# Layer 2's scores: the linear part of leaky relu as a sum per node, a one-operation relu, and a fixed order of three engines

## The chip, the cores and the metric

The kernel runs on one core of one Trainium2 chip. The metric is device time in microseconds (us): the median of several executions of the whole program, which holds four graph layers. One execution was also recorded by the hardware profiler; all views below are of that one.

## What is computed

The input x has 128 graphs of 64 nodes with 256 features. Four layers follow each other, each as `x = layernorm(x + layer(x))`. The change touches layer 2 and the end of layer 1 that is worked off beside it. Layer 2 is graph attention over 512 edges with four heads of 64 features:

```python
Xq = (H @ W_lin.T).reshape(bt, n, h, dh)
Xv = (H @ W_val.T).reshape(bt, n, h, dh)
e = jnp.einsum('behd,hd->beh', jax.nn.leaky_relu(Xq[:, src] + Xq[:, dst], 0.2), a)
e = e + jnp.log(A0[src, dst] + EPS)[None, :, None]
# softmax over the edges of one source, then
Y = segment_sum(attn[..., None] * Xv[:, dst], src)
out = Y @ W_out.T
```

The scores `e` need, for each graph, edge and head, a weighted sum over 64 features of a leaky relu. The last step of layer 1 is `x = layernorm(x + batchnorm(...))`; its batch norm is applied in a last pass over the nodes.

## The kernel before

**Tiles.** A tile of X holds two graphs: 128 partitions are 2 x 64 nodes, 256 features lie along the free axis. There are NT = 64 tiles. The scores take them as K = 32 pairs of tiles, in two halves of HU = 16 pairs; one half of the scores of one feature half `c` is one PSUM bank `sc`.

**One pair k of the scores** (`scores`, L2169) runs over these steps:

- `transposed(k)` (L2131) transposes the two tiles on TensorE into a bank `m`; VectorE copies it to `xT` (L2138).
- `maps(k)` (L2141) multiplies with the joint weights `wqv` (L2148, full 128x128 array): 256 columns are the queries, 256 the values. ScalarE copies the queries in a rounded form (`xh`, L2153), VectorE subtracts that from the bank to get the rest (`xl`, L2154), so that the edge matmuls can run as two passes of the fast float32 form. ScalarE copies the values to `xv` (L2165, two buffers), and SP's queue stores them to DRAM (L2166).
- `edges(c)` (L2182), once for each feature half: sixteen matmuls per pair (L2188, array split into 64x128) add the query vectors of the two ends of each edge, with the one-hot table `GG`. ScalarE copies each of four banks `l` to `xs` (L2194) and VectorE applies the leaky relu in place, `max(0.2 x, x)` (L2195).
- `products` (L2113) contracts `xs` over the features with the column table `az` (L2124, array split into 128x32, four at a time), and adds into `sc`.

**PSUM.** `m` has two banks, `l` two buffers of two banks each, `sc` two banks.

**What runs beside it.** In the first 16 pairs the last pass of layer 1 goes along as a generator `last_pass` (L2032): for each of 32 steps h, ScalarE applies the batch norm (`y`, L2039), TensorE transposes y back into a bank `m` (L2048), VectorE adds it to X (L1350), takes the statistics (L1353, L1354) and the root (`inv_sqrt`: a sum, ScalarE's square root at L1274, then a reciprocal, a product, a sum and a reciprocal on VectorE at L1275 to L1278, then the shift at L1365), and ScalarE scales X (L1369). Class `Norm` (L1337) holds this: `add` joins and collects, `flush` takes the root and scales. After pair 15 the softmax of the first half runs beside the scores, after that the fetch of its attention matrix `M` (L2285, on the queues of SP and GpSimd), and for the last seven pairs the first steps of `values` (mixing L2312, output map L2335). Layer 3 follows.

**What sets the order.** A scheduler orders each engine's instructions by its own estimate; `in_order` and `after` pin single ones. Semaphores between engines follow from the tiles that are read and written. Each engine then works its list strictly in order, and a queue issues its transfers in order.

## Time and profile before

| | us |
|---|---|
| median of 3 runs (2225.84 to 2228.0) | 2227.03 |
| the profiled execution, its time | 2226.54 |
| its span | 2224.8 |

Over the span TensorE is busy 2169.1 us (97%), VectorE 1831.2 (82%), ScalarE 940.3 (42%), GpSimd 162.9 (7%). By stages, busy us of each engine:

| stretch of the span, us | TensorE | VectorE | ScalarE | GpSimd |
|---|---|---|---|---|
| 0 to 1673, layers 0 and 1 | 1650.1 | 1397.8 | 546.9 | 79.5 |
| 1673 to 1840, scores with last pass | 163.3 | 144.1 | 139.2 | 1.8 |
| 1840 to 2026, scores with softmax and first values | 174.5 | 138.3 | 122.7 | 14.8 |
| 2026 to 2225, values and layer 3 | 181.2 | 151.0 | 131.4 | 66.7 |

In a line of the profile's groups or its timeline stand the engine, the line of the kernel, the operation, what it writes and reads, and sizes as partitions x elements. In the timeline, equal instructions that follow each other are merged (x4), the first two numbers are the start and the time from the first one's start to the last one's end, and a bracket gives the engine's idle time just before and what ended it. Float32 matmuls appear as two passes each.

### The profile page before, as it was taken

How to read it: one execution, taken by the hardware profiler on the slowest of the kernel's cores; microseconds unless marked ns; L12 is line 12 of the kernel's file. 1: busy time of each engine (PE TensorE's matmuls, PEld its weight loads, DVE VectorE, ACT ScalarE, POOL GpSimd, SP SyncE). 2: the span in 40 equal slices, each digit the busy share in tenths (PEclk: the TensorE clock that was granted, in tenths of full speed). 3: DMA queues.
4: the chain of work that ended last, by engine and by line, in shares of the span. 5: the costliest groups of instructions: out<-in, count | busy, mean ns of one | idle time of the engine just before them, and what ended most of it. 6: DMA issues, size and time to landing. Idle time of an engine off the chain costs nothing. (4 is left out here: it accounts for less than half of the span.)

```text
span 2224.8 us, 30044 instructions
## 1 busy us (share of the span) xinstructions
PE 2169.1 (97%) x8816; PEld 1212.6 (55%) x8816; DVE 1831.2 (82%) x9347; ACT 940.3 (42%) x1729; POOL 162.9 (7%) x196
## 2 busy tenths in 40 slices
PE   8999999999999999999999999999999999999997
PEld 6545665445665445665444654554434443446887
DVE  5788887888898899889899899787968888766788
ACT  1432322433322333332333222334437886667675
POOL 0111111101000000000000000000000000101532
PEclk9999999999999999999999999999999999999999
DMA  7000010111010111010111000012210010411522
GB/s 236 22 20 38 1 39 1 38 38 57 1 39 1 39 38 57 1 39 1 38 39 57 1 20 19 1 74 95 76 58 20 29 42 29 108 50 42 159 84 80
DMA packets 44668, 101.56 MB, mean 46 GB/s; under 512 B 5296, under 2 KB 23856, under 8 KB 43216
## 3 DMA queue, kind: packets, MB, share of 16 engines
q1 hardware_dynamic: 38384, 84.64, 11.0%
q0 software_dynamic: 3984, 14.40, 2.3%
q8 instruction: 70, 1.15, 0.2%
q10 hardware_dynamic: 2128, 0.54, 0.1%
q14 instruction: 102, 0.84, 0.1%
HBM read 67.97 MB, written 31.59 MB: 45 GB/s over the span
## 5 line engine op out<-in xcount | busy, mean ns | idle before, releaser
L1740 PE MATMUL pq<-H,wi 128*128 128x512 f32 (+1 forms) x1952 | 780.6, 540 | 1.5 <-ACT gate L1780 1.3
L1780 ACT ACTIVATE gate<-pq,bl 128x512 f32<-128x512 f32 (+1 forms) x504 | 315.8, 632 | 614.3 <-PE pq L1756 500.5
L1740 PEld LDWEIGHTS pq<-H,wi 128*128 128x128 f32 x1952 | 365.5, 190 | 336.8 <-issue 270.0
L1756 PE MATMUL pq<-lh,wh 128*128 128x512 f32 (+1 forms) x1152 | 461.3, 528 | 0.9 <-DVE lh L1798 0.8
L1756 PEld LDWEIGHTS pq<-lh,wh 128*128 128x128 f32 x1152 | 218.4, 190 | 202.5 <-issue 143.5
L1783 ACT ACTIVATE gate<-lc 128x512 f32<-128x512 f32 (+1 forms) x144 | 83.6, 581 | 278.8 <-DVE lc L1795 103.2
L2195 DVE SCALAR_TENSOR_TENSOR xs<-xs 128x512 f32<-128x512 f32 x256 | 165.3, 679 | 18.2 <-ACT xs L2194 15.1
L2194 ACT COPY xs<-l 128x512 f32<-128x512 f32 x256 | 135.6, 597 | 36.5 <-PE l L2188 30.4
L2148 PE MATMUL m<-wqv,xT 128*128 128x512 f32 (+1 forms) x264 | 123.1, 599 | 2.9 <-DVE xT L2138 1.3
L2012 PE MATMUL ps<-h,w 128*128 128x512 f32 x256 | 114.5, 604 | 5.0 <-ACT h L2006 2.7
L1369 ACT ACTIVATE X<-X,ln_sh,ln_rs 128x256 f32<-128x256 f32 x187 | 97.5, 594 | 37.1 <-DVE ln_sh L1365 21.2
L1958 PE MATMUL ps<-at,w 128*128 128x512 f32 x256 | 113.1, 593 | 0.0
L803 POOL PARTITION_ALL_REDUCE qQ<-qSG x62 | 74.0, 1193 | 508.5 <-DVE pc L135 268.9
L2012 PEld LDWEIGHTS ps<-h,w 128*128 128x128 f32 x256 | 48.3, 192 | 65.1 <-issue 55.1
L2148 PEld LDWEIGHTS m<-wqv,xT 128*128 128x128 f32 x264 | 46.0, 189 | 65.3 <-issue 39.8
L1958 PEld LDWEIGHTS ps<-at,w 128*128 128x128 f32 x256 | 47.2, 190 | 52.8 <-issue 51.4
L1353 DVE BATCH_NORM_STATS2 ln_st<-X 128x6 f32<-128x256 f32 x192 | 73.9, 415 | 1.2
L2124 PE MATMUL sc<-xs,az 128*32 128x512 f32 x512 | 74.5, 612 | 0.1
L131 DVE SCALAR_TENSOR_TENSOR CS<-GA,qE 64x1 f32<-64x1 f32 x294 | 61.8, 210 | 9.5
L1798 DVE TENSOR_TENSOR lh<-gate 128x512 f32<-128x512 f32 (+1 forms) x72 | 43.1, 602 | 31.5 <-ACT gate L1780 31.5
L131 DVE SCALAR_TENSOR_TENSOR GA<-qtg,CS,GA 64x1 f32<-64x1 f32 x294 | 61.6, 209 | 8.4
L1959 DVE BATCH_NORM_STATS2 st<-ps 128x6 f32<-128x512 f32 x64 | 43.8, 684 | 26.9 <-PE ps L1958 26.9
(637 smaller groups left out, 3452.0 us busy)
## 6 DMA issues: line engine op xcount, KB each, us to landing
wi<-in_WihT_dram SPq DMA_DIRECT2D x16, 1024.0 KB, 4.8
wh<-in_WhhT_dram SPq DMA_DIRECT2D x12, 1024.0 KB, 6.1
xd<-X SPq DMA_DIRECT2D x16, 512.0 KB, 2.6
X<-xd SPq DMA_DIRECT2D x16, 512.0 KB, 3.4
xv<-xv SPq DMA_DIRECT2D x32, 256.0 KB, 2.0
xr<-xv POOLq DMA_DIRECT2D x32, 256.0 KB, 3.0
X<-in_x_dram SPq DMA_DIRECT2D x15, 512.0 KB, 8.9
out_dram<-X SPq DMA_DIRECT2D x15, 512.0 KB, 2.9
```

Of the source, the lines that this page charges most:

```text
L131: self.nc.vector.scalar_tensor_tensor(o, a, s, b, op0, op1)
L1369: nc.scalar.activation(x, x, AF.Identity, bias=sh[:, k : k + 1], scale=rs[:, k : k + 1])
L1740: te.matmul(ps, wi[:, kk, o * P : (o + 1) * P], at(kk, k), start=(kk == 0), stop=(k == 0 and kk == 1))
L1756: te.matmul(ahead[gt, c], wh[:, kk, o * P : (o + 1) * P], hst[:, kk, :M], start=False, stop=(kk == 1))
L1780: s.activation(gates[gt][:, c, :M], ps, AF.Tanh if gt == 2 else AF.Sigmoid, bias=bl[:, p - 1, o : o + 1])
L1783: s.activation(*due.pop())
L1958: te.matmul(ps, w1[:, k, c * P : (c + 1) * P], at[:, k, :], start=(k == 0), stop=(k == 1))
L2012: te.matmul(ys[c], w2[:, k, c * P : (c + 1) * P], h[:, k, :], start=(k == 2), stop=(k == 1))
L2124: mms.append(te.matmul(sc[half][c][q : q + 32, :], az[:, c, HU - 1 - u_ : 3 * HU - 1 - u_], xs[b, i], start=(u_ == 0), stop=(u_ == HU - 1)))
L2148: te.matmul(pss[i][:, cols], xT[:, i, c, :], wqv[:, c, cols], start=(c == 0), stop=(c == 1))
L2194: taken.setdefault(i, []).append(s.copy(x, pl[:, b, :]))
L2195: ready.append(v.scalar_tensor_tensor(x, x, 0.2, x, ALU.mult, ALU.max))
```

## The change

The leaky relu is split as 0.8 relu(x) + 0.2 x. The factor 0.8 goes into `az`. The linear part needs no edges: for each node the queries are multiplied with the attention vector `a` on GpSimd (`arow`), summed per head on VectorE (`lin`), and once per half and feature half one matmul with the edge table adds 0.2 times these sums to the scores (`linear`). The relu is then one operation that reads PSUM: on ScalarE for the first graph of each tile (relu), on VectorE for the second (maximum with 0). Two more copies of the queries on ScalarE (`whole`) feed the sums.

`follow` ties each instruction of the scores to the one ahead of it on its engine, so that TensorE, ScalarE and VectorE work in the order in which the code stands. `last_pass` is no generator any more but hands out its parts, which `scores` places by hand: one pair is edges, transposes, maps, transposes, edges, and sixteen products, so the array changes its tile size four times a pair. `Norm` is split into `join`, `stats` and `root`, which returns the scalings to be placed later. Buffers: `xv` one instead of two, `xT` two instead of one, the queries' two parts three column blocks each instead of four buffers, `l` four single banks.

```diff
+    def root(self, dve=0):
+
+        nc, n, todo, mv = self.nc, len(self.todo), self.todo, self.mv
         rs = self.pool.tile([P, self.n], F32, tag="ln_rs", name="ln_rs")
...
+        return [lambda a=(k, t): scaled(*a) for k, t in enumerate(todo)]
...
-        y = normed(0)
-        for h in range(2 * NQ):
-            ps = pp.tile([P, 512], F32, tag="m", name="m")
+        y = {}
+
+        def turned(h):
+
+            ps, x = pp.tile([P, 512], F32, tag="m", name="m"), y.pop(h)
             for i in range(2):
                 for c in range(2):
-                    te.transpose(ps[:, i * D + c * P : i * D + (c + 1) * P], y[:, c, i * P : (i + 1) * P], ident)
-            with in_order(v, h < 3):
-                ln.add(2 * h, ps, 2)
+                    te.transpose(ps[:, i * D + c * P : i * D + (c + 1) * P], x[:, c, i * P : (i + 1) * P], ident)
+            ln.join(2 * h, ps, 2)
+
+        def prepare(h):
+
+            if h < 2 * NQ:
+                with in_order(s, True):
+                    y[h] = normed(h)
+
+        def whole(h):
+
+            with in_order(v, True):
+                turned(h)
+                ln.stats(2 * h, 2)
             if h == 1:
-                keep_awake(pg.tile([P, 2, 512], F32, tag="l", name="l")[:, 0, :], 2)
...
+                keep_awake(pg.tile([P, 512], F32, tag="l", name="l", bufs=4), 2)
+            prepare(h + 1)
+            with in_order(s, True), in_order(v, True):
+                ln.flush()
+
+        prepare(0)
+        return ln, turned, prepare, whole
...
-                v.tensor_tensor(az[:, c, o : o + 1], heads[:, h : h + 1], acol[:, c : c + 1], ALU.mult)
+                v.scalar_tensor_tensor(az[:, c, o : o + 1], heads[:, h : h + 1], 0.8, acol[:, c : c + 1], ALU.mult, ALU.mult)
+        arow = sx.tile([P, D], F32, tag="arow", name="arow", bufs=1)
+        ps = pp.tile([P, 512], F32, tag="m", name="m")
+        for c in range(2):
+            te.matmul(ps[:, c * P : (c + 1) * P], acol[:, c : c + 1].to_broadcast([P, P]), ident, start=True, stop=True)
+        v.tensor_copy(arow, ps[:, :D])
+        lin = sx.tile([P, 2, 2, 2, 2, HU], F32, tag="lin", name="lin", bufs=1)
+        linb = sx.tile([P, 2, 2, 2, 2, HU], F32, tag="linb", name="linb", bufs=1)
+        v.memset(linb, 0.0)
...
+        def follow(make, *a, eng=te, **k):
+
+            turn = next(i for i in reversed(nc.cur_bb.bb.instructions) if i.engine == eng.engine)
+            ins = make(*a, **k)
+            tc.add_manual_dep(ins.ins, turn.name, mybir.DependencyInfo(
+                mybir.DependencyClass.NoSync, mybir.DependencyReason.DATA), reason="turn")
+            return ins
+
+        def linear(half, c):
+
+            for b in range(2):
+                r = slice(b * N, (b + 1) * N)
+                v.tensor_scalar(linb[r, c, b], lin[r, half, c], 0.2, None, ALU.mult)
+            follow(te.matmul, sc[half][c], linb[:, c].rearrange("p b i h u -> p (b i h u)"), GG, start=False, stop=False)
...
+                if u_ == HU - 1:
+                    linear(half, c)
                 for b in range(2):
                     for i in range(2):
                         q = 32 * (2 * b + i)
-                        mms.append(te.matmul(sc[half][c][q : q + 32, :], az[:, c, HU - 1 - u_ : 3 * HU - 1 - u_],
+                        mms.append(follow(te.matmul, sc[half][c][q : q + 32, :], az[:, c, HU - 1 - u_ : 3 * HU - 1 - u_],
                                              xs[b, i], start=(u_ == 0), stop=(u_ == HU - 1)))
...
+                    follow(te.transpose, ps[:, i * D + c * P : i * D + (c + 1) * P], X[:, 2 * k + i, c * P : (c + 1) * P], ident)
+            xT = sx.tile([P, 2, 2, P], F32, tag="xT", name="xT", bufs=2)
...
+        parts = [[sx.tile([P, 3, P], F32R, tag=f"x{q}{i}", name=f"x{q}{i}", bufs=1) for q in "lh"] for i in range(2)]
+        sums, later = [], []
+
         def maps(k, xT, apart=False):
 
-            xq, xv = [], sx.tile([P, 2, D], F32, tag="xv", name="xv")
+            xq, whole, xv = [], sx.tile([P, 2, D], F32, tag="xq", name="xq", bufs=1), sx.tile([P, 2, D], F32, tag="xv", name="xv", bufs=1)
...
-                hi = sx.tile([P, D], F32R, tag="xh", name="xh", bufs=4)
-                lo = sx.tile([P, D], F32R, tag="xl", name="xl", bufs=4)
-                drawn[i] = s.copy(hi, pss[i][:, :D])
-                v.tensor_tensor(lo, pss[i][:, :D], hi.bitcast(F32), ALU.subtract)
+                lo, hi = (parts[i][q][:, :: k % 2 + 1][:, :2] for q in range(2))
+                x = pss[i][:, :D].rearrange("p (c d) -> p c d", c=2)
+                w = whole[:, i, :].rearrange("p (c d) -> p c d", c=2)
+                drawn[i] = follow(s.copy, hi, x, eng=s)
+                follow(s.copy, w, x, eng=s)
+                follow(v.tensor_tensor, lo, w, hi.bitcast(F32), ALU.subtract, eng=v)
                 xq.append((lo, hi))
...
                 product(i, slice(D, 2 * D) if apart else slice(0, 2 * D))
                 if not apart:
                     first(i)
-                s.copy(xv[:, i, :], pss[i][:, D:])
+                follow(s.copy, xv[:, i, :], pss[i][:, D:], eng=s)
+                nc.gpsimd.tensor_tensor(whole[:, i, :], whole[:, i, :], arow, ALU.mult)
+                yield
+            sums.append(lambda: follow(
+                v.tensor_reduce, lin[:, k // HU, :, :, :, k % HU].rearrange("p c i h -> p i c h"),
+                whole.rearrange("p i (c h d) -> p i c h d", c=2, h=2), AX.X, ALU.add, eng=v))
             nc.sync.dma_start(xvd[k], xv)
-            return xq
+            yield xq
 
         def scores():
 
 
             K = NT // 2
             xT = transposed(0)
-            xq = maps(0, xT, True)
-            next(beside[0])
-            next(beside[0])
+            *_, xq = maps(0, xT, True)
+            whole(2)
             xT = transposed(1)
 
+            def scales(n):
+
+                with in_order(s, True):
+                    while n and later:
+                        later.pop(0)()
+                        n -= 1
 
             held = {}
 
             def edges(c):
                 xs, ready = {}, []
                 for i in range(2):
-                    pl = pg.tile([P, 2, 512], F32, tag="l", name="l")
+                    pl = [pg.tile([P, 512], F32, tag="l", name="l", bufs=4) for _ in range(2)]
                     for part, b in ((0, 0), (0, 1), (1, 0), (1, 1)):
                         r = slice(b * N, (b + 1) * N)
-                        mm = te.matmul(pl[:, b, :], xq[i][part][r, c * P : (c + 1) * P], GGr[r, :],
+                        mm = follow(te.matmul, pl[b], xq[i][part][r, c, :], GGr[r, :],
                                        start=(part == 0), stop=(part == 1))
                         if not b and not part:
                             after(mm, taken.pop(i, []) + ([drawn[i]] if c == 0 else []))
                     for b in range(2):
                         x = xs[b, i] = sx.tile([P, E], F32, tag="xs", name="xs", bufs=10)
-                        taken.setdefault(i, []).append(s.copy(x, pl[:, b, :]))
-                        ready.append(v.scalar_tensor_tensor(x, x, 0.2, x, ALU.mult, ALU.max))
+                        y = (follow(v.tensor_scalar, x, pl[b], 0.0, None, ALU.max, eng=v) if b
+                             else follow(s.activation, x, pl[b], AF.Relu, eng=s))
+                        taken.setdefault(i, []).append(y)
+                        ready.append(y)
                 held[k, c] = xs, ready
-                last.append(mm)
 
             for k in range(K):
-                apart, xn = k < NQ, None
+                hb, ha = (h if h < 2 * NQ else None for h in (2 * k + 3, 2 * k + 4))
                 edges(0)
-                if apart:
-                    run(*beside)
-                    if k:
-                        products([(k - 1, 1)], held)
-                if k < K - 1:
-                    xn = maps(k + 1, xT)
-                if apart:
-                    run(*beside)
-                elif k < K - 2:
+                while sums:
+                    sums.pop()()
+                if ha:
+                    prepare(ha)
+                scales(2)
+                steps = maps(k + 1, xT) if k < K - 1 else iter((None,) * 3)
+                if k < K - 2:
                     xT = transposed(k + 2)
+                if hb:
+                    with in_order(v, True):
+                        turned(hb)
+                        ln.stats(2 * hb, 2)
+                next(steps)
+                scales(2)
+                next(steps)
+                xn = next(steps)
+                if ha:
+                    with in_order(v, True):
+                        turned(ha)
                 edges(1)
+                if ha:
+                    with in_order(v, True):
+                        ln.stats(2 * ha, 2)
+                products([(k - 1, 1), (k, 0)] if k else [(k, 0)], held)
+                if ha:
+                    prepare(ha + 1)
+                if hb:
+                    with in_order(v, True), in_order(s, True):
+                        later.extend(ln.root())
+                    if k in (0, NQ - 2):
+                        scales(4)
                 xq = xn
-                if apart:
-                    run(*beside)
-                    products([(k, 0)], held)
-                    xT = transposed(k + 2)
-                    run(*beside)
-                else:
-                    products([(k - 1, 1), (k, 0)], held)
                 if k == K - 1:
                     products([(k, 1)], held)
                 yield
...
+        sc_ = scores()
+        ln, turned, prepare, whole = last_pass()
+        whole(0)
+        whole(1)
         run(*[sc_] * (NQ - 1))
```

## The prediction

> **What bounds the kernel now.** I read the windows first, to see which engine is full in which stage, then the timeline of TensorE, VectorE and ScalarE for single pairs of layer 2's scores, then the waits of the DMA queue. The scores run from 1683 to 2026 us of the span. In their first half each pair also carries two steps of layer 1's last pass:
>
> ```profile
> core 0: us, PE busy (x) PEld busy (x) DVE busy (x) ACT busy (x) POOL busy (x), PEclk, DMA share, GB/s
> 1700.00:1750.00 50.00, 49.64 (x239) 20.27 (x237) 43.26 (x126) 43.56 (x100) 0.00 (x0) 1.00 0.06 22
> ```
>
> TensorE is busy 49.64 of 50 us and sets the pace; VectorE (43.3) and ScalarE (43.6) have some slack. The first maps of pairs 2 to 15 start at 1699.26 to 1839.41: thirteen periods in 140.15 us, 10.78 each. The timeline shows where one such period goes:
>
> ```profile
> 1742.56 1.98 PE L2148 MATMUL m<-wqv,xT 128*128 128x512 f32 x4
> 1744.47 0.50 PE L2188 MATMUL l<-edge_s,xl 64*128 64x512 f32 x2
> 1744.81 0.40 PE L2188 MATMUL l<-edge_s,xh 64*128 64x512 f32 x2
> 1745.04 0.39 PE L2188 MATMUL l<-edge_s,xl 64*128 64x512 f32 x2
> ...
> 1752.81 1.98 PE L2148 MATMUL m<-wqv,xT 128*128 128x512 f32 x4
> ```
>
> Edge matmuls follow each other 0.23 us apart (1744.81 to 1745.04), but the first couple after another tile size takes 0.34 (1744.47 to 1744.81). In this period the array's tile size changes ten times. The second half, without last pass, already has four changes a pair:
>
> ```profile
> 1884.83 0.50 PE L2188 MATMUL l<-edge_s,xl 64*128 64x512 f32 x2
> ...
> 1885.94 3.70 PE L2148 MATMUL m<-wqv,xT 128*128 128x512 f32 x8
> 1889.52 0.66 PE L2136 MATMUL m<-ident,X 128*128 128x128 f32 x4
> 1890.10 0.50 PE L2188 MATMUL l<-edge_s,xl 64*128 64x512 f32 x2
> ...
> 1891.23 1.92 PE L2124 MATMUL sc<-xs,az 128*32 128x512 f32 x16
> 1893.08 1.09 PE L2251 MATMUL m<-ident,se 128*128 128x128 f32 x8
> ```
>
> From starts: edges of one half E 1.12, maps M 3.58, transposes of X TX 0.58, sixteen products P 1.85; a y transpose TY beside other 128x128 work 0.52 (eight take 1.03).
>
> **Changes whose cost is plain.** *Tile order.* A first-half pair becomes E, TX, TY, M, TY, E, P: 1.12 + 0.58 + 0.52 + 3.58 + 0.52 + 1.12 + 1.85 = 9.3 us, 1.5 less than 10.78, if nothing waits. The second half keeps its order.
> *Elementwise work.* Eight copies (0.51 start to start) on ScalarE and eight operations L2195 (0.61) on VectorE become four relus and four maxima read from PSUM, plus two copies (0.27) on ScalarE and one reduction on VectorE. ScalarE: -8x0.51 + 4x0.55 + 2x0.27 = -1.3 us a pair. VectorE: -8x0.61 + 4x0.60 + 0.60 = -1.9. Neither bounds a pair now, so this alone gives nothing. A relu from PSUM is not in these rows; the gate row L1780 (128x512, 632 ns) and the copy L2194 (597) bound it. A maximum from PSUM lies between L1552 (from SBUF, 484 ns) and the copy L2138 (from PSUM, 677); I take L2138, 0.60 start to start. The reduction: L1551, 683 ns for the same 128x512.
> *GpSimd* gets two 128x256 products a pair (727 ns, row L2404). They end some 5 us before the reduction that waits for them; the DMA issues queued behind them on that queue are the scatters of the attention, which end about 0.2 to 1.5 us later.
> *The linear sum* adds four matmuls of 128x128x512 (two passes of 0.46): 0.9 us each, two before pair 17, two at the end: +2 at the end, and +1 net for pairs 14 to 24, where softmax operations now stand ahead of the xT copy but 2.8 us of TensorE idling on VectorE's backlog (0.52 + 0.51 + 0.46 + 1.28) shrink. The factor 0.8 in az costs nothing: same instructions.
>
> **The wait that the fixed order adds.** The two m banks are handed out in turn to TX, TY, M0, M1, TY: five uses a pair. M0, the first half of the maps, so takes the bank of the TX just before it, and the built program has it wait for that bank's reader, the copy xT for the pair after next. VectorE runs strictly: maximum, maximum, lin reduction, xT copy, join, statistics, lo, lo, join, maximum, maximum, statistics, then the six small operations of the normalization's root in a row. Before, the scheduler put those between other operations. Alone, they show their latency:
>
> ```profile
> 1676.27 0.17 DVE L1272 TENSOR_SCALAR is_t<-ln_mv 128x2 f32<-128x2 f32 x1
> 1676.71 0.17 DVE L1275 RECIPROCAL is_r<-is_s 128x2 f32<-128x2 f32 x1 [0.27 <-ACT is_s L1274]
> ...
> 1677.50 0.16 DVE L1365 SCALAR_TENSOR_TENSOR ln_sh<-ln_mv,ln_rs 128x2 f32<-128x2 f32 x1
> 1677.58 0.68 DVE L1350 TENSOR_TENSOR X<-m,X 128x512 f32<-128x512 f32 x1
> ```
>
> 1.31 us until the next operation (1676.27 to 1677.58), and 1.0 for two statistics and aggregates ahead of them (1675.27 to 1676.27). Now one loop, counted from the start of M0. M1 ends at 3.6. ScalarE's hi copy starts at 3.85, its second copy ends at 4.5. VectorE: second lo to 4.85, join to 5.45 (0.60), first maximum to 6.05. The second maximum and relu reuse xs buffers that the first four products of this pair still read: TensorE reaches P at 3.58 + 0.52 + 1.12 = 5.2 and eight passes take 1.06, so it runs from 6.3 to 6.9. Statistics to 7.9, root to 9.2, two maxima of the next E to 10.4, reduction to 11.0, xT copy to 11.7, semaphore 0.06: the next M0 starts at 11.8. TensorE had been ready at 9.3. So it idles 2.5 us a pair and VectorE's chain becomes the bound. Thirteen periods: 13 x (11.8 - 10.78) = **+13 us**. With the maxima at 0.48 and the reduction at 0.4 the period is 11.2, with 0.68 and 0.75 it is 12.2: +5 to +18.
>
> **The clock.** An idle stretch like this one has a price in the trace:
>
> ```profile
> 1664.72 5.40 PE L2012 MATMUL ps<-h,w 128*128 128x512 f32 x8 [2.19 <-issue]
> 1666.00:1668.00 2.00, 2.00 (x3) 0.66 (x2) 1.59 (x7) 0.20 (x1) 0.00 (x0) 0.50 0.02 4
> ```
>
> After 2.19 us idle the granted clock was 0.50, and eight matmuls that took 3.70 us just before took 5.40: 1.7 us lost. An idle of 2.73 us (before 1549.99) brought no drop, so it depends on how the idle lies in a recurring period. The drops begin whole multiples of 3.41 us apart in the records (the one at 1664.84 us, the later ones at 1948.15 and 2043.72). If 2.19 us must fall into one such period, 2.5 us of idle does so in (3.41 + 2.5 - 2x2.19)/3.41 = 45% of pairs; if 1.6 us is enough (1.56 at 1620 us was not), in 79%. The slow clock then falls on M, which is in the loop: 13 x 0.45 x 1.7 = **+10**, up to +17; none if the chain is shorter. [...]
>
> **Start.** The three whole steps ahead run their roots in VectorE's order: two of 1.31 us more stand before an xT copy than did, and the first loop's wait: M0 of pair 1 some 4 us later (0 to 5): **+4**.
>
> **One xv buffer instead of two.** The waits name the price:
>
> ```profile
> 1927.20 2.39 SPq L2285 DMA_DIRECT2D M<-attn_d  x4
> 1929.69 21.05 SPq L2166 DMA_DIRECT2D xv<-xv  x3
> 1948.88 0.37 ACT L2165 COPY xv<-m 128x256 f32<-128x256 f32 x1 [4.45 <-DMA xv<-xv]
> 1949.30 1.12 PE L2136 MATMUL m<-ident,X 128*128 128x128 f32 x4 [3.62 <-ACT xv L2165]
> ```
>
> The store of pair 24's xv stands behind the fetch of M on SP's queue and lands at about 1948.9. With two buffers pair 26 waited for it, 4.45 us. With one, pair 25 does. Its copy would start 2.5 us after its maps (1932.98), so it waits about 13 us, and the relus behind it on ScalarE hold the edge banks. TensorE still has E and P, then idles some 10.6 instead of 3.6: **+7** (0 if the store lands early, 10 at most). The slow clock after it is there in both.
>
> **Values.** In pairs 27 to 31 a join, statistics and every second time a root (0.6 + 1.0, + 1.3) stand ahead of the maxima and the xT copy, on which here M1 waits: copy done at 4.2 or 5.5 us after E starts, TensorE there at 3.5. Mean stall 1.4, less the 0.45 that present waits beyond yT's cost: +0.95 x 5 = **+5** (0 to 7). After 2026 us TensorE is the bound in both.
>
> **Sum.** 4 + 13 + 10 + 1 + 7 + 5 + 2 = +42 on the span of 2224.8; the run lay 1.7 above its span (2226.5), and the median of the runs is 2227.0: 2227 + 42 = **2269 us**.
>
> **Rivals.**
> A, *faster*: the xT copy comes in time, TensorE stays the bound at 9.3 us. Then 13 x (9.3 - 10.78) = -19 and start, clock and values cost nothing: -19 + 1 + 7 + 2 = -9, 2218 us. For it: VectorE's and ScalarE's sums fall. Against: the loop from the second lo to M0 would have to shrink from 7.3 to 4.8 us. It decides from a period of 10.0, which earns the 10 us of the rest (10.78 - 10/13).
> B, *the chain without the clock*: 11.3 us and no drop: 4 + 7 + 1 + 7 + 5 + 2 = +26, 2253. For it: 2.73 us once went free.
> C, *the slow clock nearly each pair, often for two periods of 3.41 us* (as at 1948): 13 x 0.8 x 3.3 = 34 for 10: 2293.
> D, *it does not do what it says*, the stall eating just the saved changes: period 9.7, -14 + 15: 2228.
>
> **How the numbers follow.** Forecast 52% (its own range 2258 to 2280), B 22%, C 14%, A 8%, D 4%. The range reaches into B and C: 2240 to 2290. Under 0.2% (about 4.5 us) a measurement of this kernel can't tell a change from none: faster 0.08, same 0.03, slower 0.89.
>
> **What would show it.** Right: PE idle of 2 to 3 us before each M0 of the first half, released by the xT copy; periods near 11.8 to 13.5; PEclk 0.5 in part of the slices; one xv wait of 12 us or more on ScalarE. Wrong: first-half periods under 10.5, or the xT copy ending before TY does; a first half that is warm and a loss that lies in the second.

## The result, and the profile after

| | before | after |
|---|---|---|
| median, us (range) | 2227.5 (2225.8 to 2228.5) | 2281.3 (2277.2 to 2285.5) |
| the profiled execution, its time | 2226.54 | 2277.24 |
| its span | 2224.8 | 2275.5 |

The changed kernel is slower: the ratio is 1.0242, with a 95% interval of 1.0223 to 1.0262. The prediction was 2269, with a range of 2240 to 2290; the 2281.3 lies inside it, and just above the 2258 to 2280 that the forecast gave as its own.

The windows of the changed kernel, cut at the same steps as the table of before (layers 0 and 1; scores with last pass; scores with softmax and values; the rest), with the start of pair 15's maps as the second cut. Columns: length, busy time of each engine, granted clock, DMA.

```profile
core 0: us, PE busy (x) PEld busy (x) DVE busy (x) ACT busy (x) POOL busy (x), PEclk, DMA share, GB/s
0.00:1673.00 1673.00, 1649.93 (x5136) 900.82 (x5136) 1398.00 (x8155) 547.00 (x886) 79.55 (x76) 1.00 0.11 39
1673.00:1882.80 209.80, 167.43 (x783) 82.13 (x783) 134.81 (x384) 122.97 (x288) 23.70 (x33) 0.87 0.07 25
1882.80:2078.20 195.40, 175.73 (x1089) 81.55 (x1087) 106.45 (x212) 93.26 (x214) 38.70 (x52) 0.97 0.20 56
2078.20:2275.50 197.30, 181.56 (x1824) 162.04 (x1824) 149.92 (x514) 131.32 (x275) 67.07 (x99) 0.97 0.35 99
```

The scores' first half took 209.8 us instead of 167, the second 195.4 instead of 186, the last stage 1.5 us less. In the first half TensorE works nearly as long as before (167.4 against 163.3 us, part of it now at half the clock), but with 42 us of gaps around it, and VectorE and ScalarE, whose work fell by 9 and 16 us, are idle more than before. So no engine is full: a chain of waits sets the pace. And the granted clock is 0.87, where it was 1.00.

The timeline of TensorE shows one period (in the records of this kernel all operations that went through `follow` carry line 2150, so one reads them by their tiles):

```profile
1762.49 5.40 PE L2150 MATMUL m<-wqv,xT 128*128 128x512 f32 x8 [2.52 <-DVE xT L2150]
...
1771.23 0.50 PE L2150 MATMUL l<-edge_s,xl 64*128 64x512 f32 x2
...
1772.36 0.66 PE L2150 MATMUL m<-ident,X 128*128 128x128 f32 x4
1772.85 0.60 PE L2066 MATMUL m<-ident,y 128*128 128x128 f32 x4
1775.97 5.40 PE L2150 MATMUL m<-wqv,xT 128*128 128x512 f32 x8 [2.52 <-DVE xT L2150]
...
1816.46 3.70 PE L2150 MATMUL m<-wqv,xT 128*128 128x512 f32 x8 [2.52 <-DVE xT L2150]
```

In the pair shown TensorE has its transposes done at 1773.4 and then idles 2.52 us, as in every pair from 3 to 15, until the xT copy frees the bank. The eight map matmuls then take 5.40 us instead of 3.70. A period, from the start of one pair's maps to the start of the next pair's, is 13.48 us here (1762.49 to 1775.97). Of pairs 3 to 15, pair 10's maps (1816.46) alone have the full clock, and the next maps start 11.78 us later, at 1828.24.

The timeline of VectorE over the same pair is the chain, from the second lo (`xl`, the rest of the second half's queries) to the xT copy:

```profile
1768.60 0.43 DVE L2150 TENSOR_TENSOR xl<-xq,xh 128x256 fp32r<-128x256 f32 x1 [2.00 <-ACT xq L2150]
1768.95 0.68 DVE L1353 TENSOR_TENSOR X<-m,X 128x512 f32<-128x512 f32 x1
1769.55 0.68 DVE L2150 TENSOR_SCALAR xs<-l 128x512 f32<-128x512 f32 x1
1770.50 0.69 DVE L2150 TENSOR_SCALAR xs<-l 128x512 f32<-128x512 f32 x1 [0.27 <-PE sc L2150]
1771.11 0.74 DVE L1362 BATCH_NORM_STATS2 ln_st<-X 128x6 f32<-128x256 f32 x2
1771.77 0.30 DVE L1363 BATCH_NORM_AGGREGATE ln_mv<-ln_st 128x2 f32<-128x6 f32 x2
1772.10 0.17 DVE L1272 TENSOR_SCALAR is_t<-ln_mv 128x4 f32<-128x4 f32 x1
...
1773.44 1.28 DVE L2150 TENSOR_SCALAR xs<-l 128x512 f32<-128x512 f32 x2
1774.64 0.68 DVE L2150 TENSOR_REDUCE lin<-xq 128x8 f32<-128x512 f32 x1
1775.23 0.68 DVE L2150 COPY xT<-m 128x512 f32<-128x512 f32 x1
```

From 1772.10 to 1773.44 stand the six small operations of the root, and in that time the maxima of the next pair wait, whose banks TensorE had filled by 1772.4. Behind the list's first line, which waits 2.00 us for ScalarE's copy of the maps, nothing in it waits long for another engine (0.27 us at the second maximum, and 0.27 us inside the root); it is simply a list.

The clock, in windows of 1 us over the same stretch:

```profile
1774.00:1775.00 1.00, 0.00 (x0) 0.00 (x0) 1.00 (x3) 1.00 (x3) 0.00 (x0) 1.00 0.00 0
...
1776.00:1777.00 1.00, 1.00 (x3) 0.52 (x4) 0.96 (x3) 0.00 (x0) 0.00 (x0) 1.00 0.00 0
1777.00:1778.00 1.00, 1.00 (x3) 0.49 (x2) 0.52 (x3) 0.00 (x0) 0.00 (x0) 0.52 0.00 0
1778.00:1779.00 1.00, 1.00 (x2) 0.34 (x2) 0.00 (x0) 0.18 (x1) 0.00 (x0) 0.50 0.00 0
...
1781.00:1782.00 1.00, 1.00 (x7) 0.63 (x7) 0.00 (x0) 0.60 (x3) 0.00 (x0) 1.00 0.00 0
```

The drop to 0.50 does not come in the idle stretch (1773.4 to 1776.0), but a microsecond after its end, when TensorE is busy again, and it lasts some 3.4 us. It falls on the maps, which are the next link of the chain.

Why pair 10 is spared shows in windows that are cut at the drops. Where the granted clock falls in this trace, it falls at whole multiples of 3.41 us from the other drops (1777.05, 1804.35 and 1828.25 are 8 and 7 multiples apart), and in pairs 3 to 15 it stays down for one such stretch. Here are pairs 7, 9 and 10, each with the stretch of 3.41 us ahead of a possible drop and the stretch behind it:

```profile
1773.63:1777.05 3.42, 1.08 (x3) 0.60 (x4) 3.38 (x7) 1.81 (x4) 0.00 (x0) 1.00 0.00 0
1777.05:1780.46 3.41, 3.41 (x6) 1.35 (x5) 0.89 (x4) 1.65 (x5) 0.46 (x1) 0.50 0.00 0
1800.94:1804.35 3.41, 1.38 (x3) 0.68 (x4) 3.38 (x9) 1.50 (x4) 0.00 (x0) 1.00 0.00 0
1804.35:1807.77 3.42, 3.42 (x5) 1.35 (x4) 0.59 (x3) 1.90 (x5) 0.73 (x1) 0.50 0.00 0
1814.59:1818.01 3.42, 1.55 (x4) 0.84 (x5) 3.38 (x9) 1.34 (x3) 0.00 (x0) 1.00 0.00 0
1818.01:1821.42 3.41, 3.41 (x18) 1.77 (x16) 0.84 (x3) 2.85 (x9) 0.73 (x1) 1.00 0.00 0
```

The idle is 2.52 us in all three pairs, but the part of it that lies inside one stretch shrinks from pair to pair: 2.34 us in pair 7, 2.03 in pair 9, 1.87 in pair 10 (3.42 less 1.55). After 2.03 us the clock halved, after 1.87 it did not.

By starts of the maps, after minus before, the whole +50.7 us of the span divides so: +9.0 at pair 2; +33.8 from pair 2 to 15; +2.7 from 15 to 25; +2.3 from 25 to 27; +4.4 from 27 to 31; -1.5 from there to the end.

### The profile page after: what moved, and what is told of

The parts are those of the page before. It is cut to its first block, busy times and chain, and to the rows that moved or that the text cites. A ratio compares the mean times of both kernels' runs of the same rounds, so it can differ in the third digit from the quotient of the medians.

```text
span 2275.5 us, 30057 instructions
## 1 busy us (share of the span) xinstructions
PE 2174.7 (96%) x8828; PEld 1226.5 (54%) x8828; DVE 1789.2 (79%) x9261; ACT 894.5 (39%) x1663; POOL 209.0 (9%) x260
## 3 DMA queue, kind: packets, MB, share of 16 engines
q1 hardware_dynamic: 38384, 84.64, 10.8%
## 5 line engine op out<-in xcount | busy, mean ns | idle before, releaser
L2150 PE MATMUL m<-wqv,xT 128*128 128x512 f32 (+1 forms) x264 | 146.9, 704 | 46.0 <-DVE xT L2150 42.3
L2150 PEld LDWEIGHTS m<-wqv,xT 128*128 128x128 f32 x264 | 56.3, 228 | 115.7 <-DVE xT L2150 57.0
L2150 DVE TENSOR_TENSOR xl<-xq,xh 128x256 fp32r<-128x256 f32 x64 | 27.7, 433 | 111.0 <-ACT xq L2150 110.4
L2150 DVE TENSOR_SCALAR xs<-l 128x512 f32<-128x512 f32 x128 | 84.7, 683 | 20.0 <-PE sc L2150 11.2
L2150 ACT ACTIVATE xs<-l 128x512 f32<-128x512 f32 x128 | 73.4, 598 | 46.7 <-PE sc L2150 25.6
L2221 POOL TENSOR_TENSOR xq<-xq,arow 128x256 f32<-128x256 f32 x64 | 47.0, 735 | 434.1 <-DVE xl L2150 434.1
```

What stands on the lines that cost most here:

```text
L2150: ins = make(*a, **k)
L2221: nc.gpsimd.tensor_tensor(whole[:, i, :], whole[:, i, :], arow, ALU.mult)
```

## The experiments

Unless said otherwise each is the changed kernel with one edit. Times between chips differ (the kernel before had medians of 2222 to 2228 us), so ratios to it on the same chip are given, and for parts the spans and the starts of the maps. Differences of spans carry that spread between chips, some 5 us; starts within one trace do not.

**TensorE's gap filled.** The transposes ahead of the maps are given several times, into the same bank from the same data; VectorE's list does not change.

```diff
-            for i in range(2):
+            for i in [0, 1] * n:
...
-                        turned(hb)
+                        turned(hb, 5 if k else 1)
```

> The changed kernel with the four transposes that stand just ahead of the maps in pairs 1 to 14 given five times instead of once (same bank, same data): they fill 2.1 of the 2.52 us in which TensorE idles before the first half of the maps. VectorE's chain is not touched. Theory (the idle itself costs nothing more than 11.78 - 10.78 a pair, the rest is the slow clock that it brings): period 11.8, the eight map matmuls 3.70 instead of 5.40 in every pair, granted clock 1.0 from 1682 to 1830: 12 x 1.7 = 20 us less, 2261. Rival 1 (the slow clock comes from something else in the pair, such as the array's tile sizes or VectorE's load): period stays 13.5, 2281. Rival 2 (transposes longer than the gap, M0 late): period above 11.8 with a full clock, 2265 or more.

The ratio was 1.0169 (1.0152 to 1.0186), the span 2257.8, 17.7 us less. Its TensorE timeline:

```profile
1778.55 2.35 PE L2066 MATMUL m<-ident,y 128*128 128x128 f32 x20
1781.66 3.70 PE L2150 MATMUL m<-wqv,xT 128*128 128x512 f32 x8 [0.77 <-DVE xT L2150]
...
1790.35 2.35 PE L2066 MATMUL m<-ident,y 128*128 128x128 f32 x20
1793.46 2.84 PE L2150 MATMUL m<-wqv,xT 128*128 128x512 f32 x6 [0.76 <-DVE xT L2150]
```

The period is 11.79 us (the mean of pairs 3 to 15), the maps of each of them take 3.70 us, the granted clock is 1.00 from 1720 to 1860, and the maps still start on the xT copy. More work for TensorE made the kernel faster. So the period of 13.49 is a chain of 11.78 and 1.71 of slow clock, and the slow clock comes from the gap. With three and with two times the transposes:

> The changed kernel with the same four transposes given three times instead of five, so that about 1.65 us of idle is left before the maps (0.77 with five, 2.52 with one). If an idle stretch must reach about 2.2 us within one period of 3.41 us of the throttle: no pair drops, period 11.8, 2261, as with five. If 1.4 us in such a period is enough (what 12 slow pairs of 13 would give for phases that fall at random), about two pairs in three drop, period 12.9 in the mean, 2275. If every idle over 1.2 us is enough: period 13.5, 2281.

Ratio 1.0154 (1.0137 to 1.0171), span 2258.4: with 1.65 us idle the maps of pairs 3 to 9 take 3.70 us each, and the span is within 0.6 us of that with five times the transposes.

> The changed kernel with the four transposes ahead of the maps given twice, which leaves about 2.1 us of idle (1.65 with three brought no slow pair, 2.52 with one brought 12 of 13). If at least about 2.2 us must fall into one period of the throttle: no slow pair, period 11.8, 2261. If the bound lies between 1.7 and 2.1: the idle meets it at some phases; a slow pair moves the phase by only 0.16 us, a warm one by 1.5, so slow pairs come in rows, 5 to 11 of 13, mean period 12.5 to 13.3, 2270 to 2279.

Ratio 1.0258 (1.0241 to 1.0275), no gain at all. Its timeline of TensorE:

```profile
1789.10 5.40 PE L2150 MATMUL m<-wqv,xT 128*128 128x512 f32 x8 [2.08 <-DVE xT L2150]
1802.58 3.70 PE L2150 MATMUL m<-wqv,xT 128*128 128x512 f32 x8 [2.08 <-DVE xT L2150]
1814.37 5.36 PE L2150 MATMUL m<-wqv,xT 128*128 128x512 f32 x8 [2.08 <-DVE xT L2150]
```

With 2.08 us idle, 11 of the 13 pairs 3 to 15 are slow (maps of 5.36 to 5.40 us instead of 3.70); the warm ones are pair 3 and pair 9, with five slow ones between. So the bound for these periods lies between 1.65 and 2.08 us, not at 2.19 as the prediction took it: 0.43 us of idle decide over some 20 us.

**The root taken later.** The root of pairs 1 to 13 is taken in the next pair, behind the join that follows the xT copy.

```diff
                         turned(hb)
+                        if 1 < k < NQ - 1:
+                            with in_order(s, True):
+                                later.extend(ln.root())
                         ln.stats(2 * hb, 2)
...
-                if hb:
+                if k in (0, NQ - 2):
                     with in_order(v, True), in_order(s, True):
                         later.extend(ln.root())
-                    if k in (0, NQ - 2):
-                        scales(4)
+                    scales(4)
```

> The changed kernel with the normalization's root of pairs 1 to 13 taken in the next pair, behind the join that follows the xT copy, so that its six small operations (1.3 us) no longer stand between the products and the next xT copy. Theory (VectorE's strict chain sets the pair): chain 11.78 - 1.3 = 10.5, TensorE idles about 1.2 us before the maps; if that idle no longer halves the clock, 12 x (13.49 - 10.5) = 36 us less, 2245; if it still does, period 12.2, 16 us less, 2265. Rival (the six operations only lie in a wait that is there anyway, for the scores' bank or the relus): period 13.5, no change, 2281.

Ratio 1.0094 (1.0078 to 1.0111), span 2239.5: 36.0 us less. The timeline of TensorE:

```profile
1762.37 3.70 PE L2150 MATMUL m<-wqv,xT 128*128 128x512 f32 x8 [1.11 <-DVE xT L2150]
1772.75 2.84 PE L2150 MATMUL m<-wqv,xT 128*128 128x512 f32 x6 [1.11 <-DVE xT L2150]
```

The period is 10.39, the idle 1.11 us, the granted clock 1.00 (1720 to 1840). Six operations of 0.16 to 0.18 us each, moved behind the xT copy, are worth 3.1 us a pair: 1.39 of chain and 1.71 of clock.

**The transposes of X moved behind the maps**, so that the maps no longer share a bank with the xT copy just ahead.

```diff
-                if k < K - 2:
-                    xT = transposed(k + 2)
                 if hb:
...
                 xn = next(steps)
+                if k < K - 2:
+                    xT = transposed(k + 2)
```

> The changed kernel with the transposes of X and their xT copy moved from ahead of the maps to behind them, nothing else. The banks then fall so that the first half of the maps waits for the join of the pair before, and the second half for this pair's first join; the xT copy has most of a pair. Theory (the wait for the xT copy through the shared bank is what the fixed order adds): the idle before the first half of the maps is gone and one of about 1 us stands before the second half; period 10.3 if the clock then stays full, 13 x 3.1 = 40 us less, 2241; 12 if it is still slow in each pair, 2262. Rival (VectorE's total work of a pair sets the pace, not this one wait): period 11.8 or more, at best the clock's 20 us less, 2261.

Ratio 1.0093 (1.0076 to 1.011), span 2244.3: 31.2 us less where 40 was expected. The wait did go, and a shorter one came in its place, as the timeline of TensorE shows:

```profile
1759.49 1.88 PE L2150 MATMUL m<-wqv,xT 128*128 128x512 f32 x4
1762.60 0.70 PE L2150 MATMUL m<-wqv,xT 128*128 128x512 f32 x1 [1.23 <-DVE X L1353]
```

The second half of the maps waits 1.23 us for the first join. The period is 11.3 and not 10.3: the new loop runs through the second half of the maps itself, which delays the second lo and all that follows it; the expectation had counted the lo from the start of the first half. It starts better too: pair 2's maps are 3.4 us late instead of 9.0.

**Without the ties.** `follow` no longer adds a dependence; arithmetic, buffers and code stay.

```diff
             ins = make(*a, **k)
-            tc.add_manual_dep(ins.ins, turn.name, mybir.DependencyInfo(
-                mybir.DependencyClass.NoSync, mybir.DependencyReason.DATA), reason="turn")
             return ins
```

> The changed kernel without the ties that hold each scores instruction behind the one ahead of it on its engine: same arithmetic, same buffers, same code order as priorities, and the scheduler orders the engines. Theory (the strict order of VectorE makes the xT copy late): the scheduler puts the xT copy and the joins ahead of the root's small operations, so the period falls to 10.4 to 11.3 and the clock is full in most pairs: 2242 to 2255. Rival (the bank order alone does it: the first half of the maps takes the bank of the transposes just ahead, whatever the order): period 11.8 to 13.5, 2262 to 2281.

Ratio 1.0033 (1.0023 to 1.0042), span 2230.7, better than the theory said. From pair 2 to 15 it takes 139.6 us, the kernel before 140.2, the changed kernel 173.9. The scheduler puts products between the maps and the transposes, and from pair 3 on the xT copy is awaited for at most 0.51 us. So the loss in the loop belongs to the fixed order, and the new arithmetic, with the new buffers, gains nothing in the loop when the scheduler orders it, as the prediction had it for the arithmetic. Pair 2 is 8.6 us late here as well, so the start's loss is not the ties'.

**One xv buffer, alone**, in the kernel before.

```diff
-sx.tile([P, 2, D], F32, tag="xv", name="xv")
+sx.tile([P, 2, D], F32, tag="xv", name="xv", bufs=1)
```

> The kernel before with one xv buffer instead of two, nothing else. The prediction priced this at 7 us (0 to 10): the copy of pair 25 waits about 13 us, TensorE idles 10.6 instead of 3.6. What the changed kernel's trace shows (a wait of 10.41 us, 6.13 us of TensorE's idle in place of 3.62 one pair later) says 2 to 3 us there, and 3 more at pair 29 where TensorE waits 3.69 us for xv. So 3 to 6 us over the kernel before; 0 to 1 if only the pair in which the wait lies moves.

Ratio 1.0032 (1.0019 to 1.0045), which is 7 us; the span of 2233.5 is 8.7 us more, on another chip. The first line is its ScalarE, the second its TensorE:

```profile
1949.97 0.65 ACT L2165 COPY xv<-m 128x256 f32<-128x256 f32 x2 [11.05 <-DMA xv<-xv]
1950.40 1.12 PE L2136 MATMUL m<-ident,X 128*128 128x128 f32 x4 [11.15 <-ACT xv L2165]
```

TensorE idles 11.15 us; the prediction's price was 10.6 and +7. My expectation here, which had been lowered to 3 to 6 after the trace of the changed kernel, was the worse one. In the changed kernel itself the same wait looks so, on ScalarE and TensorE:

```profile
1991.41 0.37 ACT L2150 COPY xv<-m 128x256 f32<-128x256 f32 x1 [10.41 <-DMA xv<-xv]
1991.83 1.22 PE L2448 MATMUL m<-w,b 128*128 128x256 f32 x2 [6.13 <-ACT xv L2150]
```

ScalarE waits as long, but TensorE idles only 6.13 us. From pair 25 to 27 it takes 27.5 us, before 25.2, and the kernel before with one buffer 34.2. The trace has the store land 18.5 us after the fetch of M began (1972.94 to 1991.41), in the other 21.7 us (1928.26 to 1949.97): 3.2 us of the difference. What decides over that span was not tried.

**The store on another queue.**

```diff
-            nc.sync.dma_start(xvd[k], xv)
+            s.dma_start(xvd[k], xv)
```

> The changed kernel with the stores of xv issued on ScalarE's queue instead of SP's, so that none stands behind the fetch of M. One buffer as before. Theory (the wait of 10.41 us on ScalarE at pair 25 is the store queued behind M's fetch, and the one of 3.69 us on TensorE at pair 29 one behind the second fetch or its transfers): both waits fall under 1 us, 6 + 3.5 us less, and the first half loses up to 2 us where ScalarE issues the stores: 2272 to 2274. Rival 1 (the store is slow because all transfers share the 16 engines with M's fetch): the waits stay, 2281. Rival 2 (issuing on ScalarE delays its relus): above 2281.

Ratio 1.0256 (1.0239 to 1.0274), span 2277.4, no gain. Its ScalarE:

```profile
1974.14 0.34 ACTq L2226 DMA_DIRECT2D xv<-xv  x1
...
1988.37 0.37 ACT L2150 COPY xv<-m 128x256 f32<-128x256 f32 x1 [8.10 <-DMA xv<-xv]
```

Nothing stands ahead of the store on this queue, it is issued at 1974.14, and yet the copy that waits for it starts only at 1988.4, 14 us later (the median of these stores is 2.0 from issue to landing). In that time the DMA engines are full:

```profile
1974.00:1988.00 14.00, 5.58 (x36) 2.16 (x32) 4.59 (x8) 3.04 (x7) 4.32 (x7) 0.80 1.02 247
```

Their share is 1.02, with 247 GB/s, while M is fetched. So the wait is mostly not one for a place in SP's queue: counted from the start of the fetch, the copy came after 16.1 us here (1972.31 to 1988.37) and after 18.5 in the changed kernel, so that the place accounts for 2.4 us at most. The store itself takes those 14 us beside the fetch. The prediction's "stands behind the fetch of M on SP's queue" is wrong as the main mechanism; another queue doesn't mend it, another buffer does. Pair 29's wait of 3.69 us stayed as well; it was no DMA (below).

**Towards a better version.** The transposes moved, the root taken in the next pair, the join for the second half of the maps ahead of the sums, all statistics behind the maxima, and, since one xT buffer is then enough, two xv buffers. The lines that it adds to a pair, or moves there:

```diff
                 steps = maps(k + 1, xT) if k < K - 1 else iter((None,) * 3)
+                if hb:
+                    with in_order(v, True):
+                        turned(hb)
+                while sums:
+                    sums.pop()()
                 next(steps)
+                if 1 < k < NQ - 1:
+                    with in_order(v, True), in_order(s, True):
+                        later.extend(ln.root())
                 scales(2)
                 next(steps)
                 xn = next(steps)
+                if k < K - 2:
+                    xT = transposed(k + 2)
                 if ha:
                     with in_order(v, True):
                         turned(ha)
                 edges(1)
+                if hb:
+                    with in_order(v, True):
+                        ln.stats(2 * hb, 2)
```

> The changed kernel with both waits taken apart: transposes of X and xT copy behind the maps, the join for the second half of the maps ahead of the sums, the root in the next pair behind the first lo, both statistics behind the maxima; one xT buffer, and the space of the second for a second xv buffer. Theory: TensorE's 9.3 us and VectorE's 9.0 us of work a pair are nearly equal, so the period is 9.3 to 9.9 with a full clock: 13 x (11.3 - 9.6) = 22 less than with the moved transposes alone, and the second xv buffer gives 3 to 6: 2215 to 2222, about the kernel before or a little faster, since the start still costs 9. Rival (a new chain through the moved operations): period 10.4 or more, 2232 or more.

Ratio 1.0141 (1.0124 to 1.0158), 2258 us: the rival. ScalarE, then TensorE:

```profile
1782.77 1.09 ACT L1383 ACTIVATE X<-X,ln_sh,ln_rs 128x256 f32<-128x256 f32 x2 [1.15 <-DVE ln_sh L1378]
1783.76 0.35 ACT L2150 CAST xh<-m 128x256 fp32r<-128x256 f32 x1
```

```profile
1784.71 0.90 PE L2066 MATMUL m<-ident,y 128*128 128x128 f32 x4 [2.40 <-ACT xv L2150]
```

Two scalings of X wait on ScalarE for the root's last operation; the copies of the maps' second half stand behind them and hold the bank of the next transposes. TensorE idles 2.40 us, and most periods are 13.4 us, with the slow clock (edge matmuls 0.43 us apart, 1772.94 to 1773.37). The next edit puts these scalings behind the copies, and leaves out the ties from pair 27 on:

```diff
-                scales(2)
                 next(steps)
+                scales(2)
                 xn = next(steps)
```

> The rearranged kernel (transposes of X behind the maps, root in the next pair, two xv buffers) with the two scalings of X that stood between the copies of the two map halves on ScalarE put behind both, and without the ties from pair 27 on. In the rearranged kernel those scalings wait for the root's last operation, the copies behind them hold the bank of the next transposes, and TensorE idles 2.4 us a pair, at the slow clock. Theory: without that wait the period falls from 13.4 to 9.6 to 10.2 with a full clock, and the wait at pair 29 (4.5 us over the kernel before) goes: 2196 to 2212, faster than the kernel before. Rival (VectorE's and ScalarE's strict lists, 9.0 and 8.2 us of work a pair, find the next wait): 10.8 or more, 2220 or more.

Ratio 0.995 (0.9936 to 0.9963), 2214.15 us where the kernel before took 2226.07: faster than both by a small amount that the interval bears out, and a little less than expected. The period is 10.10 in each pair from pair 3 on. Its windows (scores with last pass, the rest of the scores):

```profile
1673.00:1835.00 162.00, 146.00 (x780) 70.64 (x779) 130.22 (x379) 121.46 (x283) 23.68 (x33) 0.99 0.09 30
1835.00:2015.00 180.00, 172.99 (x1100) 84.23 (x1099) 111.54 (x226) 98.17 (x223) 39.02 (x53) 0.99 0.22 63
```

Pairs 25 to 27 take 24.5 us with two xv buffers (25.2 before), and pair 29's wait is gone. Moving the other two scalings behind the first copies as well:

> As the run before, and the other two scalings of a pair moved from ahead of ScalarE's copies of the first map half to behind them. Theory: the first lo comes about 0.5 us earlier and the edges with it; 0 to 0.4 us a pair less than in the run before, 0 to 5 us. Rival (they now stand ahead of the root's square root and make the root late by 1.1 us, which VectorE's list hands on): 0.5 us a pair more, 7 us more.

Ratio 0.9961 (0.9947 to 0.9975), period 10.25: the rival, though with 0.15 us a pair instead of 0.5. The intervals of the two ratios overlap; it is the period, read in the traces, that tells them apart.

**The old arithmetic in that order.** Copy and leaky relu in place instead of relu and maximum; no sums per node, no `linear`, `az` without 0.8.

```diff
-                        y = (follow(v.tensor_scalar, x, pl[b], 0.0, None, ALU.max, eng=v) if b
-                             else follow(s.activation, x, pl[b], AF.Relu, eng=s))
-                        taken.setdefault(i, []).append(y)
-                        ready.append(y)
+                        taken.setdefault(i, []).append(follow(s.copy, x, pl[b], eng=s))
+                        ready.append(follow(v.scalar_tensor_tensor, x, x, 0.2, x, ALU.mult, ALU.max, eng=v))
```

> The order that is faster than both kernels, with the old arithmetic put back: eight copies on ScalarE and eight leaky relus in place on VectorE per pair, no sums per node, no linear matmuls. Theory (the cheaper elementwise work is worth nothing in the order of the kernel before, but carries the new one): VectorE's list grows by 1.9 us a pair to about 11, ScalarE's by 1.3, the first-half period from 10.1 to 11.5 to 12.5 and with idles over 2 us partly at the slow clock; 13 x 1.4 to 2.4 and up to 10 for the second half: 2232 to 2255. Rival (the order alone is the gain, TensorE stays the bound): period 10.1 to 10.5, 2210 to 2220.

Ratio 1.0264 (1.0243 to 1.0286), 2280 us, worse than expected: periods alternate between 12.84 and 14.45, with idles of 2.31 us before the second half of the maps. The idle is the same in each pair, and yet only every other one is slow: that half of the maps takes 3.55 us from 1739.73 and 1.98 from 1754.13. The two periods add up to 27.3 us, eight times 3.41. From the length of the slow maps the drop is put at about 1739.5 (an estimate), and the idle then lies alternately within one stretch of the grid of 3.41 us (about 2.1 us of it, and slow maps follow) and across an edge (about 1.3 and 1.0 us on its two sides, and none follow). The cheaper elementwise work gains nothing in the scheduler's order, but this fixed order, which was arranged for it, depends on it: 3% between the two.

## Why the prediction was right, and where its terms were not

- *What adds the wait.* Right, link by link: the first half of the maps waits for the xT copy through the shared bank; 2.52 us of idle where 2.5 was said. Taking the root out of the link leaves 1.11 us, taking the transposes out of it leaves none there.
- *The loop of 11.8 us, +13.* Right: 11.78 in the warm pair, 11.79 when the gap is filled; 13 x (11.78 - 10.78) = 13. TensorE's own work of 9.3 us a pair is right too: 11.78 less 2.52 of idle is 9.26.
- *The clock, +10 (up to 17).* Mis-sized: 33.8 - 13 = 20.8, since 12 of 13 pairs were slow (12 x 1.71 = 20.5) and not 45%. Two things failed in this step. The bound of 2.19 us within one stretch of 3.41 us is too high: 2.03 was enough in the changed kernel, 1.87 was not. Put with a bound of 1.95 into the prediction's own sum, idles of 2.52 us at random phases would hit some six pairs in ten (an estimate). And the idle does not fall at random: a slow pair of 13.49 us is 0.16 less than four such stretches (4 x 3.41 = 13.65), so the next idle lies nearly where the last one lay, while a warm pair of 11.78 moves it by 1.54. So slow pairs come in rows, a warm one ends a row and starts the next. The trace shows it: the drops lie on the grid, and along the row from pair 7 to pair 10 the idle inside one stretch falls from 2.34 to 1.87 us, where the row ends. The alternating periods of the last run are, by the estimate given there, the same effect. The idle of 2.73 us that brought no drop in the kernel before was no exception: the point of the grid at 1548.78, 34 stretches ahead of that trace's drop at 1664.84, cut it into 1.52 and 1.21 us. The bound is not quite sharp: ahead of the changed kernel's drop at 1705.37, 1.75 us were enough, and 1.86 us between its 1913.58 and 1916.99 were not; ahead of the drop at 2043.72 in the kernel before, 1.38 us were.
- *Start, +4.* Mis-sized: +9.0. The prediction counted the roots ahead of an xT copy (they cost 1.5 us at pair 0's maps), but not the clock there: the maps of pairs 0 and 1 took 5.46 and 6.08 us at the slow clock, behind idles of 2.23 and 2.04 us (the second, like one of 2.14 ahead of pair 2, a wait for ScalarE's scaling of X, which the prediction did not count either). With the transposes moved the term is 3.4; without the ties it is 8.6.
- *Pairs 14 to 24, +1:* +2.7 from 15 to 25.
- *One xv buffer, +7.* Right for the edit alone (+7 by ratio in the kernel before), +2.3 in the changed kernel; the mechanism was in the main named wrongly, as the run with the other queue shows.
- *Values, +5.* The sum is right (+4.4), the step is not. Not every pair lost 0.95: pair 29 lost 4.5 and the others together nothing. What blocks is not VectorE's root but ScalarE behind it, in the changed kernel's timeline:

```profile
2029.90 0.20 ACT L1274 ACTIVATE is_s<-is_t 128x4 f32<-128x4 f32 x1 [1.46 <-DVE is_t L1272]
2031.15 2.08 ACT L1383 ACTIVATE X<-X,ln_sh,ln_rs 128x256 f32<-128x256 f32 x4 [1.05 <-DVE ln_sh L1378]
2033.14 1.06 ACT L2150 ACTIVATE xs<-l 128x512 f32<-128x512 f32 x2
```

  The square root and four scalings stand ahead of the relus and of the copies of maps that had ended at 2031.4, 2.7 us before the first of these copies; TensorE idles 3.69 us for a copy. Without ties (period 11.6) it is gone.
- *The linear sum, +2 at the end.* Not seen: from pair 31's maps to the end it is -1.5.
- *Elementwise work gives nothing by itself.* Right in the scheduler's order. What the prediction did not see is that it pays in an order that is arranged around it: 10.10 us a pair with it, 12.84 and 14.45 without.
- *Rivals.* A, faster, needed a period under 10; the moved root alone gave 10.39, the rearranged kernel 10.10. B, the chain without the clock, is what the filled gap shows: 1.0154 to 1.0169 by ratio, 2262 to 2265 us, with a period of 11.79 where B took 11.3. C, with 0.8 of the pairs slow, came nearest to the 12 of 13, but each spent one stretch of 3.41 us at the slow clock, not often two. The sum of +42 against +50.7 misses by the clock (+10.8), the start (+5) and pairs 15 to 25 (+1.7), less what xv, the values and the end did not cost (-8.8). That the total came out this near is partly luck: errors of 17.5 us one way and 8.8 the other.

## What to carry to other kernels

When an order is fixed by hand, walk each engine's list as a loop and ask of every buffer that is handed out in turn whose reader frees it: a copy for the pair after next held up the maps of the next pair only because both took banks from the same two. Small operations with latency between them (a root, 1.34 us here) belong behind the copy that another engine waits for, and work that waits for them belongs behind the copies on its own engine; the rearranged order, with the second xv buffer that it makes room for, and without the ties from pair 27 on, was worth 3% here, and turned the change into a gain of 0.5%. Before a gap on TensorE is priced, look at how long it is and where it lies on the grid of the drops: in these runs one of 1.65 us cost its length alone, one of 2.08 was followed by maps of 5.36 to 5.40 us instead of 3.70 in 11 pairs of 13, and the loop locked to the grid, because its slow period of 13.49 us was nearly four times 3.41 us.

## What the runs showed of the hardware that was not expected

- An idle of 2.08 us per pair was followed by maps of 5.36 to 5.40 us instead of 3.70 in 11 pairs of 13, and one of 1.65 in none of pairs 3 to 9. In the changed kernel the granted clock falls to 0.50 up to 1.4 us after the idle has ended (0.01 us in pair 11, 1.08 in pair 7, 1.38 in pair 9), at the next point of a grid of 3.41 us, and in pairs 3 to 15 it stays there for one stretch of it.
- Twenty transposes instead of four, whose results are the same, made the kernel 18 us of span faster.
- A store of 256 KB, whose median from issue to landing is 2.0 us, needed 14 us beside the fetch of M, from a queue in which nothing stood ahead of it.
